# Second convolution with the propagation after the weights: transposes of the raw relu output in place of a matmul with S

## The chip, the cores and the metric

One core of one Trainium2 chip. The time is device time in microseconds (us), the median of several executions; a trace of one execution shows what each engine did. A core has TensorE (PE; its weight loads are PEld), VectorE (DVE), ScalarE (ACT), GpSimd (POOL) and queues for transfers. All data are FP32.

## The reference

128 graphs of 128 nodes with 512 features. Layer 0 is graph attention with a residual and a LayerNorm. Layer 1, cut to what the change touches:

```python
h = relu(hypergraph_conv(x, adj, W1, b1))        # 128 x 1024 per graph
h = layer_norm(h, gamma, beta)
y = hypergraph_conv(h, adj, W2, b2)              # 128 x 512
out = layernorm(x + (y + x))
# hypergraph_conv(x, adj, W, b) = D^-1 H B^-1 H^T (x W^T) + b
```

In the inputs gamma is one, and beta, b1 and b2 are zero.

## The kernel before

With S = H B^-1 H^T (symmetric, built once per graph) a convolution is D^-1 S (x W^T). The kernel multiplies by S first: a matmul with h as the stationary operand gives (S h)^T, which is just the layout that the product with the weights needs. The hidden layer is normalized on VectorE before that.

```python
def s7_hidden(g):
    ...                                   # ph = zT.T @ W1, h = relu(ph * D + b1)
    mv = moments(h, DH, f"h{g}")
    rs = rstd_of(mv[:, 1:2], f"h{g}")     # the power on GpSimd
    for q in range(2):                    # four VectorE passes per graph
        ... h = (h - mean) * gamma
        ... h = h * rs + beta

def s8_propagate(g):
    ...
        nc.tensor.matmul(p[:, k * N:(k + 1) * N], s["h"][:, c * P:(c + 1) * P], s["S"], ...)   # pu
    ...                                   # pu -> uT, half on ScalarE, half on VectorE

def s9_output(g):
    for k in range(KH):                   # py, 8 matmuls of 512 columns
        nc.tensor.matmul(p, s["uT"][:, k, :], w2_sb[:, k, :], ...)
    o = p * D + res; LayerNorm; store

order = (
    (s6_propagate, 2), (s4_transpose, 1), (s1_transpose, 0), (s7_hidden, 2),
    (s2_features, 0), (s3_softmax, 0), (s8_propagate, 2), (s5_attend, 1), (s9_output, 2),
)
for t in range(G + 2): ...                # stage(t - lag): three graphs in flight
```

Tile names in the traces: pz = x1 times S, pet, pt, pa = transposes, ph = first weights, pe, pd, pf = scores, S and features, ps = score matrix, pu = h times S, pav = attention, py = second weights.

## Time and profile before

| | before |
|---|---|
| time, median | 3494.22 us (3493.81 to 3496.34) |
| TensorE busy | 3447.3 us of 3493.5 |
| VectorE, ScalarE, GpSimd busy | 2251.0, 1203.7, 791.4 us |
| one loop step (start of one ph to the next) | 26.80 us |

The lines behind this stand in the prediction. A busy share of 99% does not say that nothing can be gained or lost on TensorE: the ends of matmul records are modelled and overlap the next ones. The distance between the starts of consecutive groups is what a stage costs.

### The profile page before, as it was taken

The page shows a single profiled execution, that of the slowest core. Times are in us where ns is not written, and L with a number is a line of the kernel's source. Part 1 is how long each engine was busy: PE and PEld are TensorE (multiplying, and loading weights), DVE is VectorE, ACT ScalarE, POOL GpSimd, SP SyncE. Part 2 cuts the span into 40 slices and gives each one's busy share as a digit, 9 for nine tenths or more (in the row PEclk, how much of TensorE's full clock was granted, in tenths as well). Part 3 has the DMA queues.
Part 4 walks back from the last instruction along what each step waited for, and adds up shares of the span by engine and source line. Part 5 has one row for each costly group of instructions (what it writes and reads, how often), then busy time and mean ns, then how long its engine had stood idle before and what let it go on. Part 6 is the DMA issues. An engine that isn't in the chain of part 4 may idle for free.

```text
span 3493.5 us, 39269 instructions
## 1 busy us (share of the span) xinstructions
PE 3447.3 (99%) x13952; PEld 1961.2 (56%) x13952; DVE 2251.0 (64%) x4880; ACT 1203.7 (34%) x3585; POOL 791.4 (23%) x910
## 2 busy tenths in 40 slices
PE   6999999999999999999999999999999999999998
PEld 3555555555555555555555555555555555555554
DVE  4666666666666666666666666666666666666664
ACT  2333333333333333333333333333333333333331
POOL 2222222222222222222222222222222222222221
PEclk9999999999999999999999999999999999999999
DMA  3000000000000000000000000000000000000000
GB/s 120 25 21 21 24 25 21 21 25 24 21 23 26 21 21 24 25 21 21 24 25 21 21 24 25 21 21 24 25 21 21 24 25 21 21 24 25 21 10 12
DMA packets 58596, 85.89 MB, mean 25 GB/s; under 512 B 6304, under 2 KB 22688, under 8 KB 58400
## 3 DMA queue, kind: packets, MB, share of 16 engines
q1 hardware_dynamic: 57392, 80.77, 7.0%
q8 instruction: 110, 1.80, 0.2%
q10 hardware_dynamic: 1008, 2.62, 0.2%
q14 instruction: 86, 0.70, 0.1%
HBM read 49.81 MB, written 33.55 MB: 24 GB/s over the span
## 4 chain that ended last, share of the span: by engine, by line
PE 98%; DVE 1%; DMA 0%; POOL 0%; ACT 0%; issue 0%; SPq 0%; POOLq 0%; DVEq 0%; ACTq 0%
PE py L340 25%; PE ph L299 25%; PE pf L204 13%; PE pu L326 7%; PE ps L217 7%; PE pav L262 6%; PE pe L181 4%; PE pz L285 3%; PE pet L251 3%; PE pt L154 2%; PE pd L191 2%; PE pd L192 0%; PE pa L156 0%; DMA w_sb<-in_w_dram 0%; DVE prod L114 0%
## 5 line engine op out<-in xcount | busy, mean ns | idle before, releaser
L340 PE MATMUL py<-w_sb,uT 128*128 128x512 f32 x2048 | 908.0, 596 | 0.0
L299 PE MATMUL ph<-w_sb,zT 128*128 128x512 f32 x2048 | 900.8, 593 | 0.7 <-ACT zT L290 0.7
L340 PEld LDWEIGHTS py<-w_sb,uT 128*128 128x128 f32 x2048 | 379.9, 191 | 429.2 <-issue 398.8
L299 PEld LDWEIGHTS ph<-w_sb,zT 128*128 128x128 f32 x2048 | 379.5, 190 | 429.8 <-issue 428.8
L204 PE MATMUL pf<-w_sb,xT 128*128 128x512 f32 x1024 | 473.7, 605 | 0.0
L302 DVE SCALAR_TENSOR_TENSOR h<-ph,D,b_bc 128x512 f32<-128x512 f32 x256 | 192.1, 751 | 430.4 <-PE ph L299 430.4
L239 ACT ACTIVATE e<-d,nmax 128x128 f32<-128x128 f32 x1024 | 396.1, 388 | 116.3 <-DVE nmax L232 116.3
L136 POOL TENSOR_TENSOR rs_h<-ve_h,mhalf 128x1 f32<-128x1 f32 x128 | 126.1, 985 | 1322.1 <-DVE ve_h L134 1322.1
L226 POOL TENSOR_TENSOR d<-d,neg 128x512 f32<-128x512 f32 x256 | 319.6, 1269 | 396.4 <-DVE D L199 365.9
L305 ACT ACTIVATE h<-h 128x512 f32<-128x512 f32 x256 | 161.1, 629 | 664.5 <-DVE h L302 664.5
L290 ACT COPY zT<-pz 128x512 f32<-128x512 f32 x128 | 75.0, 586 | 750.1 <-PE pz L285 750.1
L326 PEld LDWEIGHTS pu<-S,h 128*128 128x128 f32 x2048 | 241.5, 194 | 106.5 <-DVE dn L197 95.5
L144 DVE BATCH_NORM_STATS2 stats_h<-h 128x6 f32<-128x512 f32 x256 | 177.7, 694 | 178.0 <-ACT h L305 178.0
L204 PEld LDWEIGHTS pf<-w_sb,xT 128*128 128x128 f32 x1024 | 185.9, 192 | 185.3 <-issue 185.3
L326 PE MATMUL pu<-S,h 128*128 128x128 f32 x2048 | 266.0, 284 | 9.4 <-DVE h L314 9.4
L217 PE MATMUL ps<-rhs_aug,lhs_aug 40*128 40x512 f32 x512 | 253.5, 615 | 0.0
L262 PE MATMUL pav<-ft,eT 128*128 128x64 f32 x2048 | 243.5, 272 | 0.0
L262 PEld LDWEIGHTS pav<-ft,eT 128*128 128x128 f32 x2048 | 239.7, 193 | 0.8 <-PE ps L217 0.8
L225 DVE TENSOR_TENSOR d<-ps,d 128x512 f32<-128x512 f32 x256 | 176.9, 691 | 84.8 <-ACT d L224 71.8
L232 DVE TENSOR_REDUCE nmax<-d 128x4 f32<-128x512 f32 x256 | 175.5, 686 | 67.6 <-POOL d L226 67.6
L208 ACT COPY ft<-pf 128x512 f32<-128x512 f32 x128 | 74.9, 585 | 398.6 <-PE pf L204 398.6
L273 DVE SCALAR_TENSOR_TENSOR y<-y,x 128x512 f32<-128x512 f32 x128 | 88.6, 692 | 177.0 <-POOL y L272 177.0
(69 smaller groups left out, 3855.3 us busy)
## 6 DMA issues: line engine op xcount, KB each, us to landing
x<-in_x_dram SPq DMA_DIRECT2D x128, 256.0 KB, 2.6
out_dram<-o SPq DMA_DIRECT2D x128, 256.0 KB, 2.0
a<-in_adj_dram SPq DMA_DIRECT2D x128, 64.0 KB, 1.8
w_sb<-in_w1t_dram SPq DMA_DIRECT2D x1, 2048.0 KB, 13.9
w_sb<-in_w2t_dram SPq DMA_DIRECT2D x1, 2048.0 KB, 14.0
w_sb<-in_w_dram SPq DMA_DIRECT2D x1, 1024.0 KB, 11.3
b_bc<-in_b_dram ACTq DMA_DIRECT2D x2, 256.0 KB, 6.6
b_bc<-in_b_dram ACTq DMA_DIRECT2D x1, 512.0 KB, 8.5
```

Of the source, the lines that this page charges most:

```text
L144: nc.vector.bn_stats(stats[:, i, :], t[:, i * HALF:(i + 1) * HALF])
L204: nc.tensor.matmul(pf, s["xT"][:, k, :], w0_sb[:, k, :], start=(k == 0), stop=(k == KF - 1))
L217: nc.tensor.matmul(p, l, r[:, q * HH:(q + 1) * HH, :].rearrange("r h n -> r (h n)"), start=True, stop=True,)
L225: nc.vector.tensor_max(dq, ps[q], dq)
L226: nc.gpsimd.tensor_tensor(d[:, q * HH:(q + 1) * HH, :], d[:, q * HH:(q + 1) * HH, :], s["neg"][:, None, :].to_broadcast([P, HH, N]), op=AL ...
L232: nc.vector.tensor_reduce(nmax[:, q * HH:(q + 1) * HH], d[:, q * HH:(q + 1) * HH, :], AX.X, ALU.max, negate=True,)
L239: nc.scalar.activation(e[:, h, :], d[:, h, :], AF.Exp, bias=nmax[:, h:h + 1], accum_out=den[:, h:h + 1])
L262: nc.tensor.matmul(p[:, h * U:(h + 1) * U], s["eT"][:, h, :], s["ft"][:, h * U:(h + 1) * U], start=True, stop=True,)
L299: nc.tensor.matmul(p, s["zT"][:, k, :], w1_sb[:, k, cols], start=(k == 0), stop=(k == KF - 1))
L302: nc.vector.scalar_tensor_tensor(h[:, cols], p, s["D"], b1_bc[:, cols], op0=ALU.mult, op1=ALU.add)
L326: nc.tensor.matmul(p[:, k * N:(k + 1) * N], s["h"][:, c * P:(c + 1) * P], s["S"], start=True, stop=True,)
L340: nc.tensor.matmul(p, s["uT"][:, k, :], w2_sb[:, k, :], start=(k == 0), stop=(k == KH - 1))
```

## The change

The intent: take the LayerNorm of the hidden layer off the path to TensorE. With per-row mean mu and factor rs,

S LN(h) W2 = (S diag(rs)) (h (gamma W2) - mu (gamma^T W2)) + (S 1) (beta^T W2).

So the raw relu output is transposed, multiplied by w2g = gamma W2, corrected by a rank-one term for the mean (y2), and multiplied by Sr = diag(rs) S (S is symmetric) only then (pq). The beta term goes into the residual. gamma^T W2 and beta^T W2 are made once by TensorE (pv) and spread over the partitions through DRAM. The core of the diff:

```diff
 def s2_features(g):
-    nc.scalar.copy(sm, pd[:, :N])
+    nc.scalar.activation(sm, pd[:, :N], AF.Copy, accum_out=ssum)
+    nc.vector.tensor_mul(dsum, ssum, dd)
 def s5_attend(g):
-    nc.vector.scalar_tensor_tensor(res, x1, 2.0, b2_bc, op0=ALU.mult, op1=ALU.add)
+    nc.gpsimd.tensor_scalar(res, bw_bc, s["dsum"], None, op0=ALU.mult)
+    nc.gpsimd.tensor_tensor(res, res, b2_bc, op=ALU.add)
+    nc.vector.scalar_tensor_tensor(res, x1, 2.0, res, op0=ALU.mult, op1=ALU.add)
 def s7_hidden(g):
-    (four VectorE passes over h, 128 x 512 each)
+    nc.vector.tensor_scalar(nmu, mv[:, 0:1], -1.0, None, op0=ALU.mult)
+    nc.gpsimd.tensor_scalar(sr, s["S"], rs, None, op0=ALU.mult)
 (second convolution)
-    nc.tensor.matmul(p[...], s["h"][:, c * P:(c + 1) * P], s["S"], ...)      # pu, 8 per graph
+    nc.tensor.transpose(p[...], s["h"][:, c * P:(c + 1) * P], ident)         # pu, 8 per graph
-    nc.tensor.matmul(p, s["uT"][:, k, :], w2_sb[:, k, :], ...)               # py, 8 per graph
+    nc.tensor.matmul(p, s["hTh"][:, k, :], w2g[:, k, :], ...)                # py, 8 per graph
+    nc.vector.scalar_tensor_tensor(y2, gw_bc, s["nmu"], p, op0=ALU.mult, op1=ALU.add)
+    nc.tensor.matmul(p, s["Sr"], s["y2"], start=True, stop=True)             # pq, 1 per graph
-    (s6_propagate, 2), (s4_transpose, 1), (s1_transpose, 0), (s7_hidden, 2), ...
+    (s6_propagate, 2), (s10_output, 3), (s4_transpose, 1), (s1_transpose, 0), (s7_hidden, 2), ...
+    (fold(), pv and w2g, at the end of the first step)
```

More of the change, by code (lines that the diff above doesn't have):

```diff
@@ L60 @@
     work = ctx.enter_context(tc.tile_pool(name="work", bufs=2))
-    small = ctx.enter_context(tc.tile_pool(name="small", bufs=4))
+    small = ctx.enter_context(tc.tile_pool(name="small", bufs=6))
+    dram = ctx.enter_context(tc.tile_pool(name="dram", bufs=1, space=bass.MemoryType.DRAM))
     psum = ctx.enter_context(tc.tile_pool(name="psum", bufs=8, space=bass.MemoryType.PSUM))
@@ L95 @@
     b1_bc = spread(b1, DH, "b1_bc")
-    g_bc = spread(gamma, DH, "g_bc")
-    be_bc = spread(beta, DH, "be_bc")
     b2_bc = spread(b2, F, "b2_bc")
+    gb = const.tile([P, 2, KH], F32, name="gb")
+    for c, ap in ((0, gamma), (1, beta)):
+        nc.scalar.dma_start(gb[:, c, :], ap.rearrange("(k p) -> p k", p=P))
     load(2)
@@ L147, in moments, with fold @@
         return mv
+    w2g = const.tile([P, KH, F], F32, name="w2g")
+    gw_bc = const.tile([P, F], F32, name="gw_bc")
+    bw_bc = const.tile([P, F], F32, name="bw_bc")
+    def fold():
+        pv = bank("pv")
+        for k in range(KH):
+            nc.tensor.matmul(
+                pv[:2], gb[:, :, k], w2_sb[:, k, :], start=(k == 0), stop=(k == KH - 1)
+            )
+        sums = const.tile([2, F], F32, name="sums")
+        nc.vector.tensor_copy(sums, pv[:2])
+        sums_d = dram.tile([2, F], F32, tag="sums_d", name="sums_d")
+        nc.scalar.dma_start(sums_d, sums)
+        for c, t in ((0, gw_bc), (1, bw_bc)):
+            nc.scalar.dma_start(t, sums_d[c].partition_broadcast(P))
+        for k in range(KH):
+            nc.gpsimd.tensor_scalar(w2g[:, k, :], w2_sb[:, k, :], gb[:, 0, k:k + 1], None, op0=ALU.mult)
     def s1_transpose(g):
@@ L193, in s2_features @@
         sm = s["S"] = work.tile([P, N], F32, tag="S", name=f"S_{g}", bufs=4)
-        nc.scalar.copy(sm, pd[:, :N])
+        ssum = small.tile([P, 1], F32, tag="ssum", name=f"ssum_{g}")
+        nc.scalar.activation(sm, pd[:, :N], AF.Copy, accum_out=ssum)
         dn = small.tile([P, 1], F32, tag="dn", name=f"dn_{g}")
@@ L201, in s2_features @@
         )
+        dsum = s["dsum"] = small.tile([P, 1], F32, tag="dsum", name=f"dsum_{g}")
+        nc.vector.tensor_mul(dsum, ssum, dd)
         pf = bank(f"pf_{g}")
@@ L277, in s5_attend @@
         nc.vector.tensor_scalar(x1, y, mv[:, 0:1], rs, op0=ALU.subtract, op1=ALU.mult)
-        res = s["res"] = work.tile([P, F], F32, tag="res", name=f"res_{g}")
-        nc.vector.scalar_tensor_tensor(res, x1, 2.0, b2_bc, op0=ALU.mult, op1=ALU.add)
+        res = s["res"] = work.tile([P, F], F32, tag="res", name=f"res_{g}", bufs=4)
+        nc.gpsimd.tensor_scalar(res, bw_bc, s["dsum"], None, op0=ALU.mult)
+        nc.gpsimd.tensor_tensor(res, res, b2_bc, op=ALU.add)
+        nc.vector.scalar_tensor_tensor(res, x1, 2.0, res, op0=ALU.mult, op1=ALU.add)
     def s6_propagate(g):
@@ L306, in s7_hidden, with s8_transpose @@
         mv = moments(h, DH, f"h{g}")
+        nmu = s["nmu"] = small.tile([P, 1], F32, tag="nmu", name=f"nmu_{g}")
+        nc.vector.tensor_scalar(nmu, mv[:, 0:1], -1.0, None, op0=ALU.mult)
         rs = rstd_of(mv[:, 1:2], f"h{g}")
-        for q in range(2):
-            cols = slice(q * HALF, (q + 1) * HALF)
-            nc.vector.scalar_tensor_tensor(
-                h[:, cols], h[:, cols], mv[:, 0:1], g_bc[:, cols],
-                op0=ALU.subtract, op1=ALU.mult,
-            )
-            nc.vector.scalar_tensor_tensor(
-                h[:, cols], h[:, cols], rs, be_bc[:, cols], op0=ALU.mult, op1=ALU.add
-            )
-    def s8_propagate(g):
+        sr = s["Sr"] = work.tile([P, N], F32, tag="Sr", name=f"Sr_{g}")
+        nc.gpsimd.tensor_scalar(sr, s["S"], rs, None, op0=ALU.mult)
+    def s8_transpose(g):
         s = st[g]
-        uT = s["uT"] = work.tile([P, KH, N], F32, tag="uT", name=f"uT_{g}")
+        hT = s["hTh"] = work.tile([P, KH, N], F32, tag="hTh", name=f"hTh_{g}")
         per = HALF // N
@@ L325, in s8_propagate @@
                 c = q * per + k
-                nc.tensor.matmul(
-                    p[:, k * N:(k + 1) * N], s["h"][:, c * P:(c + 1) * P], s["S"],
-                    start=True, stop=True,
+                nc.tensor.transpose(
+                    p[:, k * N:(k + 1) * N], s["h"][:, c * P:(c + 1) * P], ident
                 )
-            dst = uT[:, q * per:(q + 1) * per, :].rearrange("p k n -> p (k n)")
+            dst = hT[:, q * per:(q + 1) * per, :].rearrange("p k n -> p (k n)")
             if q:
@@ L334, in s8_propagate, with s9_weights, s10_output @@
                 nc.scalar.copy(dst, p)
-    def s9_output(g):
-        s = st.pop(g)
-        p = bank(f"py_{g}")
-        for k in range(KH):
-            nc.tensor.matmul(
-                p, s["uT"][:, k, :], w2_sb[:, k, :], start=(k == 0), stop=(k == KH - 1)
-            )
+    def s9_weights(g, half):
+        s = st[g]
+        if half == 0:
+            s["py"] = bank(f"py_{g}")
+        p = s["py"]
+        for k in range(half * KH // 2, (half + 1) * KH // 2):
+            nc.tensor.matmul(
+                p, s["hTh"][:, k, :], w2g[:, k, :], start=(k == 0), stop=(k == KH - 1)
+            )
+        if half == 0:
+            return
+        y2 = s["y2"] = work.tile([P, F], F32, tag="y2", name=f"y2_{g}")
+        nc.vector.scalar_tensor_tensor(y2, gw_bc, s["nmu"], p, op0=ALU.mult, op1=ALU.add)
+    def s10_output(g):
+        s = st.pop(g)
+        p = bank(f"pq_{g}")
+        nc.tensor.matmul(p, s["Sr"], s["y2"], start=True, stop=True)
         o = work.tile([P, F], F32, tag="o", name=f"o_{g}", bufs=3)
@@ L351 @@
     order = (
-        (s6_propagate, 2), (s4_transpose, 1), (s1_transpose, 0), (s7_hidden, 2),
-        (s2_features, 0), (s3_softmax, 0), (s8_propagate, 2), (s5_attend, 1), (s9_output, 2),
+        (s6_propagate, 2), (s10_output, 3), (s4_transpose, 1), (s1_transpose, 0), (s7_hidden, 2),
+        (s2_features, 0), (s3_softmax, 0), (s8_transpose, 2), (s5_attend, 1),
+        (lambda g: s9_weights(g, 0), 2), (lambda g: s9_weights(g, 1), 2),
     )
-    for t in range(G + 2):
+    for t in range(G + 3):
         if AHEAD <= t + AHEAD - 1 < G:
@@ L360 @@
                 stage(t - lag)
+        if t == 0:
+            fold()
 def kernel(
```

## The prediction

> **What bounds the kernel now.** I read the page's busy shares first, then the chain of work that ended last, then one loop step of the timeline, engine by engine.
>
> ```profile
> PE 3447.3 (99%) x13952; PEld 1961.2 (56%) x13952; DVE 2251.0 (64%) x4880; ACT 1203.7 (34%) x3585; POOL 791.4 (23%) x910
> ...
> PE 98%; DVE 1%; DMA 0%; POOL 0%; ACT 0%; issue 0%; SPq 0%; POOLq 0%; DVEq 0%; ACTq 0%
> ```
>
> TensorE is busy 99% of the span and 98% of the chain. VectorE has 36% to spare, so what the change takes from it (four 745 ns passes per graph) buys nothing by itself. The price is set by TensorE's order and its waits. One step of the loop (one graph enters, one leaves), TensorE's rows, columns start, length, line, operation, count:
>
> ```profile
> 1734.48 1.98 PE L217 MATMUL ps<-rhs_aug,lhs_aug 40*128 40x512 f32 x4
> 1736.39 2.05 PE L326 MATMUL pu<-S,h 128*128 128x128 f32 x16
> 1738.28 1.90 PE L262 MATMUL pav<-ft,eT 128*128 128x64 f32 x16
> 1740.02 7.08 PE L340 MATMUL py<-w_sb,uT 128*128 128x512 f32 x16
> 1746.94 1.05 PE L285 MATMUL pz<-S,x 128*128 128x128 f32 x8
> 1747.83 1.04 PE L251 MATMUL pet<-ident,e 128*128 128x128 f32 x8
> 1748.70 0.60 PE L154 MATMUL pt<-ident,x 128*128 128x128 f32 x4
> 1749.14 0.27 PE L156 MATMUL pa<-ident,a 128*128 128x128 f32 x1
> 1749.25 7.03 PE L299 MATMUL ph<-w_sb,zT 128*128 128x512 f32 x16
> ```
>
> Read starts, not lengths: lengths overlap, because each includes the time until the last result is out. The previous step's ph row starts at 1722.45, so a step is 26.80 us, with no gap in it. Start to start: ps 1.91, pu 1.89, pav 1.74, py 6.92, pz 0.89, pet 0.87. A matmul is two records (pu: 8 matmuls, x16), a transpose is one (pet: 8 transposes, x8). That is the saving that the change is after.
>
> VectorE in the same step, around the end of py:
>
> ```profile
> 1744.77 0.55 DVE L277 TENSOR_SCALAR x<-y,mv_a,rs_a 128x512 f32<-128x512 f32 x1 [0.66 <-POOL rs_a L136]
> 1745.35 0.69 DVE L279 SCALAR_TENSOR_TENSOR res<-x,b_bc 128x512 f32<-128x512 f32 x1
> 1747.14 0.75 DVE L344 SCALAR_TENSOR_TENSOR o<-py,D,res 128x512 f32<-128x512 f32 x1 [1.09 <-PE py L340]
> ```
>
> The py bank can be read 0.20 us after pz has begun (1747.14 less 1746.94), and the pass takes 0.75 us.
>
> The tail, where no other graph covers the hidden layer's chain (TensorE rows):
>
> ```profile
> 3449.15 3.75 PE L326 MATMUL pu<-S,h 128*128 128x128 f32 x16 [4.74 <-DVE h L314]
> 3452.70 2.56 PE L262 MATMUL pav<-ft,eT 128*128 128x64 f32 x16
> 3455.09 7.09 PE L340 MATMUL py<-w_sb,uT 128*128 128x512 f32 x16
> ```
>
> Here TensorE stands 4.74 us behind the normalization and then runs pu at half speed (3.75 against 2.05 us). This happens for the last two graphs only.
>
> **What the Trainium skill says.** "TensorE: Matmul & The Clock Gate", section "Back-to-back issue gap", gives N/2.4 + 2.5 ns between warm matmuls. "FP8 and Floating Point Precision", section "TensorE Precision Notes", says that true FP32 takes four passes. Together they fit the trace: two records per matmul, each streaming its columns twice, make 1024/2.4 + 2.5 = 429 ns per record, and py shows 6.92/16 = 433. The first page's section "Step-by-step: what each phase is for" says that weight loads are pulled ahead of running matmuls. The trace agrees where nothing is waited for: pz's first load starts at 1746.51, before the last py record has ended. After a wait it does not: in the tail, ph waits for zT; its load and its first record both start at 3463.80 and the third load comes 0.54 us later instead of 0.43, so 0.11 us of load is exposed. Last, "Part 4: PE-mode transpose" of that page says that transposes do not count as busy for the clock. The trace does not contradict this, but its three transpose groups in a row (1.42 us) leave the granted clock at 1.00 in every steady window.
>
> **The change part by part, per step.**
> Removed: 8 matmuls h times S, 1.89 us. Added in the same place: 8 transposes. Pace as pet, 0.87, plus the first weight load behind ps, which is exposed there: 16 records at pz's pace (0.89 per 8) would be 1.78, pu takes 1.89, so 0.11. Sum 0.98. Difference -0.91 us.
> Kept: py, 8 matmuls of 512 columns, 6.92 us (w2g in place of w2).
> Added: pq, one matmul of 512 columns, two records: 6.92/8 = +0.865 us. TensorE's own balance is thus about zero, -0.05 us.
> Added: a new wait. The instruction order puts pq directly behind pz, and pq needs y2, a VectorE pass over the finished py bank. Counting from the start of pz: bank readable 0.20, pass 0.75, restart of TensorE 0.06 (zT ends 3463.74, ph's load 3463.80), exposed load 0.11: pq streams from 1.12 us. Without the wait it would stream from 0.89. +0.23 us.
> VectorE is free for y2: x1 and res hang on ps, not on py, and end 11.56 us after ps starts (1746.04 less 1734.48). In the new step py starts 0.91 us earlier; its bank is readable 1.91 + 0.98 + 1.74 + 6.92 + 0.20 = 11.75 us after ps. The slack is 0.19 us, thin.
> pz needs x1 at 11.55 after ps and gets it at 10.84: no wait.
> Hidden: VectorE loses 4 x 0.745 us and gains y2 (0.75) and two small operations (0.15 each); it should fall from 2251 to about 2030 us. GpSimd gains res (a 128x512 multiply, about 0.7 us, estimated from 297 ns for 128x128 and 1027 ns for 1024 columns; an add, 1.27) and Sr (0.30): about +2.25 us per step, to some 1080 us. They run between the hidden layer's variance (1733.1) and the masking adds (1737.0); chained they end at about 1736.1, so they fit. ScalarE's accumulation with S adds about 0.3 us, off the path.
> Step: -0.91 + 0.865 + 0.23 = +0.185 us. Over some 126 steps: +23 us.
> Start: the fold is 8 matmuls of 512 columns, 6.9 us, where TensorE now waits 3.2 us for the first softmax: about +4. The sums' round trip through DRAM also holds GpSimd's queue, because the first res waits for it ahead of the first masking and bias adds, so it may be more. 1 MB less of broadcasts while the first weights load gives perhaps 1 back. I take +4 us.
> Tail: the waits of 4.74 and 4.65 us shrink to about 1.2 each (h pass 0.75, relu 0.63, less the first bank's transposes): -7. The half-clock stretches behind them (pu 3.75 and 3.79 against 1.89, py 7.95 against 6.92, pav 0.6) go: -5.4. The last pq stands behind a fully exposed y2: +0.9 beyond what is counted. About -11.5 us.
> Sum: 3494 + 23 + 4 - 11.5 = 3509.5 us.
>
> **Rivals.**
> (a) The y2 wait is hidden, because TensorE takes up pq without exposing its load or because the bank is readable earlier. For it: only 0.06 us separates y2's end (0.95) from pz's end (0.89). Against: every stalled start in the tail shows the exposed load. Then a step is 26.75 us, and the time about 3481 us.
> (b) VectorE is late for y2: res now also waits for GpSimd, and the slack is 0.19 us. If GpSimd's three new operations push the masking adds back by 0.5 us, y2 starts about 0.3 us late: +38 us, 3547 us. Against: GpSimd is idle for 2.90 us just before those adds in the trace.
> (c) The waits that the change removes are worth more than I think: nothing in a steady step waits for the normalization now, so there is nothing to win except in the tail. I give this little.
> (d) More transposes pull the clock down. One stretch like the tail's pu (3.75 us for 1.89 us of work) in every step would cost 7%. Against: the new group lies between ps and pav, alone, 0.98 us.
>
> **Range and chances.** (a) to my sum spans 3481 to 3510; part of (b), and a start of +10, reach 3530. I predict 3509 us, 8 in 10 between 3488 and 3531. Two per cent is 70 us, or 0.55 us per step: no saving of that size exists on TensorE, so faster gets 0.01. Slower needs (b) in full and more, or (d): 0.03. Within 2%: 0.96.
>
> **What would show it.** Transposes at one record each, a step between two pu rows 0.98 us long up to pav; pz to pq 1.1 us from start to start; pq to pet about 0.97 or 0.87 (whether the exposed load is booked to pq or ahead of it); a step of 26.95 to 27.05. TensorE's busy share may hide the wait, since pz's last record is drawn until 1.05 us after its start. Waits in the tail of about 1 us for h. If pz to pq is 0.89, (a) holds; if y2 starts later than 0.25 us after pz, (b).

## The result, and the profile after

| | before | after |
|---|---|---|
| time, median | 3494.22 us | 3514.31 us (3513.83 to 3514.95, 4 runs) |
| span of the profiled run | 3493.5 us | 3512.0 us |
| one loop step (mean of 125) | 26.80 us | 27.02 us |
| VectorE busy | 2251.0 us | 1984.3 us |
| GpSimd busy | 791.4 us | 1184.3 us |

The ratio is 1.0057, 95% interval 1.0043 to 1.0071; the ratios quoted here are those of the medians quoted. The change takes 267 us of work off VectorE and makes the kernel 0.6% slower: clear of the noise, and within the 2% below which two kernels count as the same.

The page of the changed kernel, busy shares and chain of work:

```profile
PE 3462.8 (99%) x13200; PEld 1884.8 (54%) x13200; DVE 1984.3 (56%) x4753; ACT 1228.4 (35%) x3713; POOL 1184.3 (34%) x1302
...
PE 98%; issue 1%; DMA 0%; DVE 0%; POOL 0%; ACT 0%; POOLq 0%; ACTq 0%
```

TensorE is again 99% busy. New is 1% of "issue" in the chain: time that the profile puts down to nobody. One step of the timeline, TensorE:

```profile
1752.55 1.09 PE L351 MATMUL pu<-ident,h 128*128 128x128 f32 x8
1753.48 1.90 PE L289 MATMUL pav<-ft,eT 128*128 128x64 f32 x16
1755.21 7.08 PE L366 MATMUL py<-w2g,hTh 128*128 128x512 f32 x16
1762.13 1.05 PE L315 MATMUL pz<-S,x 128*128 128x128 f32 x8
1763.28 1.10 PE L377 MATMUL pq<-y,Sr 128*128 128x512 f32 x2
1764.21 1.04 PE L278 MATMUL pet<-ident,e 128*128 128x128 f32 x8
```

Start to start: pu now takes 0.93 us (1.89 before). pz has the same 8 records as before and takes 1.14 to 1.15 us to its follower, where it took 0.89. pq takes 0.93 us up to pet. No bracket marks a wait on these rows, because pz's last record is drawn until 1763.18, only 0.10 us before pq. The Trainium skill says in "Perfetto Trace Analysis", section "Tensor Engine Instruction (MATMUL, LD_WEIGHTS)", that a TensorE end time is estimated and not observed; here that estimate covers most of a wait of 0.25 us per step. The same place with all engines:

```profile
1761.78 0.69 DVE L309 SCALAR_TENSOR_TENSOR res<-x,res 128x512 f32<-128x512 f32 x1
1762.13 1.05 PE L315 MATMUL pz<-S,x 128*128 128x128 f32 x8
...
1762.39 0.74 DVE L372 SCALAR_TENSOR_TENSOR y<-gw_bc,nmu,py 128x512 f32<-128x512 f32 x1
1763.25 0.30 PEld L377 LDWEIGHTS pq<-y,Sr 128*128 128x128 f32 x2 [0.25 <-issue]
1763.28 1.10 PE L377 MATMUL pq<-y,Sr 128*128 128x512 f32 x2
```

The DVE row "y<-gw_bc" is y2. It begins 0.26 us after pz, with VectorE coming straight from res, and ends at 1763.13. Only then, 0.12 us later, does pq's weight load begin, though its operand Sr was ready long before. The wait for y2 is not on the matmul but on a separate semaphore instruction ahead of the load (51 ns, from 0.04 us after y2's end in the packed trace), so that the load is held back with the matmul. In the kernel before, the load of a group that waits for nothing stands ahead of the group (pz's at 1746.51 for 1746.94).

GpSimd in the same step:

```profile
1750.02 0.61 POOL L341 TENSOR_SCALAR Sr<-S,rs_h 128x128 f32<-128x128 f32 x1
1750.60 1.56 POOL L307 TENSOR_SCALAR res<-bw_bc,dsum 128x512 f32<-128x512 f32 x1
1752.25 1.27 POOL L308 TENSOR_TENSOR res<-res,b_bc 128x512 f32<-128x512 f32 x1
1753.48 2.50 POOL L253 TENSOR_TENSOR d<-d,neg 128x512 f32<-128x512 f32 x2
```

The masking adds (tile d) in the kernel before:

```profile
1737.04 2.49 POOL L226 TENSOR_TENSOR d<-d,neg 128x512 f32<-128x512 f32 x2 [2.90 <-DVE D L199]
```

Before, GpSimd stood idle for 2.90 us ahead of them and began them 2.56 us after ps. Now its three new operations run up to them, and they begin 2.84 us after ps (1750.64). The run res_plain below, without the two res rows, starts them at 2.56 again.

The tail, TensorE. ph and pu of the last two graphs are no longer separated by the normalization:

```profile
3474.47 0.60 PE L351 MATMUL pu<-ident,h 128*128 128x128 f32 x4
3476.33 0.66 PE L351 MATMUL pu<-ident,h 128*128 128x128 f32 x4 [1.26 <-ACT h L335]
3476.82 1.90 PE L289 MATMUL pav<-ft,eT 128*128 128x64 f32 x16
```

The wait is 1.26 us instead of 4.74 (and again 1.26 for the last graph, instead of 4.65), and the half-speed stretch behind it is gone; the granted clock was 0.50 in it before (3449.1 to 3452.5).

Where the 18.5 us between the two profiled spans (3493.5 and 3512.0) come from, all read from starts of ph rows: the first ph starts at 60.16 us before and 63.06 after (+2.9); from there to the ph of the third graph from the end it is 3350.84 us (to 3411.00) and 3378.06 us (to 3441.12), which is +27.2 over 125 steps; from there to the end 82.5 and 70.9 us (-11.6).

### The profile page after: what moved, and what is told of

The parts are those of the page before. It is cut to its first block, busy times and chain, and to the rows that moved or that the text cites. A ratio compares the mean times of both kernels' runs of the same rounds, so it can differ in the third digit from the quotient of the medians.

```text
span 3512.0 us, 38412 instructions
## 1 busy us (share of the span) xinstructions
PE 3462.8 (99%) x13200; PEld 1884.8 (54%) x13200; DVE 1984.3 (56%) x4753; ACT 1228.4 (35%) x3713; POOL 1184.3 (34%) x1302
## 4 chain that ended last, share of the span: by engine, by line
PE 98%; issue 1%; DMA 0%; DVE 0%; POOL 0%; ACT 0%; POOLq 0%; ACTq 0%
PE py L366 25%; PE ph L329 25%; PE pf L231 13%; PE ps L244 7%; PE pav L289 6%; PE pq L377 4%; PE pu L351 4%; PE pe L205 4%; PE pz L315 3%; PE pet L278 3%; PE pt L178 2%; PE pd L215 2%; PE pd L216 0%; PE pa L180 0%; PE pv L161 0%
## 5 line engine op out<-in xcount | busy, mean ns | idle before, releaser
L366 PE MATMUL py<-w2g,hTh 128*128 128x512 f32 x2048 | 906.9, 596 | 0.0
L366 PEld LDWEIGHTS py<-w2g,hTh 128*128 128x128 f32 x2048 | 379.3, 190 | 428.5 <-issue 428.1
L139 POOL TENSOR_TENSOR rs_h<-ve_h,mhalf 128x1 f32<-128x1 f32 x128 | 70.3, 549 | 1150.1 <-DVE dn L222 1134.0
L139 POOL TENSOR_TENSOR rs_o<-ve_o,mhalf 128x1 f32<-128x1 f32 x128 | 70.3, 550 | 737.4 <-DVE ew L190 716.9
L299 POOL TENSOR_TENSOR y<-y,b_bc 128x512 f32<-128x512 f32 x128 | 162.5, 1270 | 128.3 <-DVE y L294 128.1
L307 POOL TENSOR_SCALAR res<-bw_bc,dsum 128x512 f32<-128x512 f32 x128 | 200.2, 1564 | 5.1 <-DMA bw_bc<-sums_d 5.1
```

Of the source, the lines that this page charges most:

```text
L307: nc.gpsimd.tensor_scalar(res, bw_bc, s["dsum"], None, op0=ALU.mult)
L366: nc.tensor.matmul(p, s["hTh"][:, k, :], w2g[:, k, :], start=(k == 0), stop=(k == KH - 1))
```

## The experiments

Theory 1: the loss is the wait of pq for y2, together with the weight load that this wait exposes, in the place where pq stands; without it the change would gain. Rivals: pq costs its 1.2 us wherever it stands; or GpSimd's new work is what delays y2 and is the whole loss.

**pq_later.** The same kernel, pq two groups later:

```diff
-    (s6_propagate, 2), (s10_output, 3), (s4_transpose, 1), (s1_transpose, 0), (s7_hidden, 2),
+    (s6_propagate, 2), (s4_transpose, 1), (s1_transpose, 0), (s10_output, 3), (s7_hidden, 2),
```

> The last propagation (pq) moves from behind pz to behind the transposes of x and adj, so that y2 has 2.3 us from the start of pz instead of 0.9. Theory 1 (the loss is the wait for y2, with the weight load that it exposes): pz to its follower falls from 1.14 to 0.89 us, pq costs 0.87 instead of 0.93, the step falls from 27.03 to 26.71 us, the time by 126 x 0.32 = 40 us to about 3474 us, below the kernel before. Rival (pq costs its 1.2 us wherever it stands, through its own operand load or its place in the PSUM rotation): step 27.0, 3514 us.

Measured: 3473.87 us, against 3494.18 for the kernel before on the same chip (ratio 0.9942, 0.9925 to 0.9958). TensorE in one step:

```profile
1743.30 1.05 PE L315 MATMUL pz<-S,x 128*128 128x128 f32 x8
1744.19 1.04 PE L278 MATMUL pet<-ident,e 128*128 128x128 f32 x8
1745.07 0.60 PE L178 MATMUL pt<-ident,x 128*128 128x128 f32 x4
1745.50 0.27 PE L180 MATMUL pa<-ident,a 128*128 128x128 f32 x1
1745.61 1.02 PE L377 MATMUL pq<-y,Sr 128*128 128x512 f32 x2
1746.47 7.03 PE L329 MATMUL ph<-w_sb,zT 128*128 128x512 f32 x16
```

pz takes 0.89 again, pq 0.86, the step 26.70 us (the ph before starts at 1719.77). Moving pq (with the VectorE passes of the output, which wait for it) behind 1.4 us of other work gives 40 us and turns a loss of 0.6% into a gain of 0.6%. The rival on pq's own cost falls. So the wait costs 0.32 us per step: 0.25 between pz and pq, 0.07 as a slower start of pq.

**res_plain.** The two GpSimd operations of the residual are left out (res = 2 x1 + b2 again). This is right with these inputs, because beta is zero, and wrong in general.

```diff
-    nc.gpsimd.tensor_scalar(res, bw_bc, s["dsum"], None, op0=ALU.mult)
-    nc.gpsimd.tensor_tensor(res, res, b2_bc, op=ALU.add)
-    nc.vector.scalar_tensor_tensor(res, x1, 2.0, res, op0=ALU.mult, op1=ALU.add)
+    nc.vector.scalar_tensor_tensor(res, x1, 2.0, b2_bc, op0=ALU.mult, op1=ALU.add)
```

> GpSimd's two operations for the residual are left out (res = 2 x1 + b2 again; right here because beta is zero, wrong in general). pq keeps its place. Theory 1: GpSimd delays y2 by only 0.05 us per step, so pz to pq falls from 1.14 to about 1.09 us and the time by some 6 us, plus about 4 us at the start, because the first residual no longer waits for the sums' round trip: 3504 us. Rival 2 (GpSimd's backlog is the whole wait): pz to pq falls to 0.89 us, the time to about 3478 us.

Measured: 3505.74 us (ratio to before 1.0033), so 8.6 us less than the change. VectorE and TensorE at pq:

```profile
1730.41 1.05 PE L313 MATMUL pz<-S,x 128*128 128x128 f32 x8
...
1730.62 0.75 DVE L370 SCALAR_TENSOR_TENSOR y<-gw_bc,nmu,py 128x512 f32<-128x512 f32 x1 [0.16 <-PE py L364]
1731.48 0.30 PEld L375 LDWEIGHTS pq<-y,Sr 128*128 128x128 f32 x2 [0.20 <-issue]
1731.51 1.10 PE L375 MATMUL pq<-y,Sr 128*128 128x512 f32 x2
```

y2 now waits for py itself (0.16 us) and starts 0.21 us after pz; pz to pq is 1.10 us. GpSimd's backlog is worth 0.04 us per step (1.14 to 1.10), 4.4 us over the 125 steps, and the first ph starts at 60.18 instead of 63.06 us. Together that is the 7.3 us by which the two profiled spans differ. As the whole cause this rival falls: 0.21 of the 0.25 us stay.

**sr_vector.** Sr on VectorE, so that pq waits for one engine only.

```diff
-    nc.gpsimd.tensor_scalar(sr, s["S"], rs, None, op0=ALU.mult)
+    nc.vector.tensor_scalar(sr, s["S"], rs, None, op0=ALU.mult)
```

> Sr is made on VectorE instead of GpSimd, so pq waits for one engine instead of two; res stays on GpSimd. Theory 1: the second wait costs a separate semaphore instruction of 0.05 us, and GpSimd's masking adds come 0.6 us earlier, which takes away the 0.05 us by which y2 is late: pz to pq about 1.03 us instead of 1.14, 12 to 14 us in all, about 3501 us. Rival: the semaphore instruction runs ahead and costs nothing, then pz to pq stays at 1.09 and the time at about 3508 us.

Measured: 3501.22 us (ratio to before 1.0020). TensorE at pq:

```profile
1729.56 1.05 PE L315 MATMUL pz<-S,x 128*128 128x128 f32 x8
...
1730.56 0.30 PEld L377 LDWEIGHTS pq<-y,Sr 128*128 128x128 f32 x2
1730.56 1.12 PE L377 MATMUL pq<-y,Sr 128*128 128x512 f32 x2
1731.52 1.04 PE L278 MATMUL pet<-ident,e 128*128 128x128 f32 x8
```

y2 starts 0.20 us after pz (1729.76) and ends at 1730.51; the load follows 0.05 us later. In res_plain it follows 0.11 us after y2's end (1731.37). The difference is the separate semaphore instruction, which the traces show once per pq (128 of 51 ns each) with two waits, and not with one; here the wait for y2 is on the load itself. The exposed weight load stays: pq takes 0.96 us here up to pet, 0.10 more than in pq_later. The gain has two parts: y2 begins 0.05 us earlier (without Sr ahead of them, GpSimd's masking adds begin 2.65 and not 2.84 us after ps), and the hand-over from y2's end to the load is 0.06 us shorter. What is left of the wait is 0.21 us: this run has the conditions that the prediction assumed, and it put the wait at 0.23.

**y2_twice.** The suspected wait lengthened: VectorE copies y2 onto itself once more before pq may read it.

```diff
     nc.vector.scalar_tensor_tensor(y2, gw_bc, s["nmu"], p, op0=ALU.mult, op1=ALU.add)
+    nc.vector.tensor_copy(y2, y2)
```

> y2 is copied onto itself on VectorE once more before pq may read it (0.55 to 0.6 us). If the wait for y2 stands in the path one to one, the step grows by that much, to about 27.6 us, and the time by 70 to 76 us, to about 3588 us. If TensorE had slack at pq, the time stays at 3514 us.

Measured: 3572.57 us, one look, +58.3. The size was missed, because the copy takes 0.43 us, not 0.55. pz to pq grows from 1.14 to 1.60, by 0.46; 126 times that is 58 us. The slope is the one that theory 1 asks for: y2's chain lies on the path one to one.

**no_pq.** One part of the change alone, with a wrong result: the output is taken from y2 without the last propagation.

```diff
-    p = bank(f"pq_{g}")
-    nc.tensor.matmul(p, s["Sr"], s["y2"], start=True, stop=True)
+    p = s["y2"]
```

> Wrong result on purpose: the last propagation is left out, the output is taken from y2 directly. What remains of the change on TensorE is transposes in place of h times S. Theory 1: the step is 27.03 - 1.14 - 0.93 + 0.89 = 25.85 us, 0.95 below the kernel before, and the time about 3514 - 126 x 1.18 - 2 = 3363 us: TensorE sets the step alone, and the change gives the whole saving back for one 512-column matmul and its wait. Rival: with TensorE relieved, the chain over VectorE and GpSimd (y, x1, res), which already delays the first weight load of pz, becomes the bound, and the step stays above 26.2 us (over 3405 us).

Measured: 3364.05 us (one look), step 25.84 us. The transposes save 0.96 us per step, and nothing but TensorE binds down to a step of 25.84 us: against the 27.02 us of the changed kernel the other engines have at least 1.18 us to spare. In the correct kernel pq takes 0.86 of these 0.96 back by its own work alone.

**row_terms_vector.** Towards a better version: pq in the late place, the beta row and rs in a second VectorE pass over y2, S itself as pq's operand; GpSimd loses Sr and both residual operations.

```diff
     nc.vector.scalar_tensor_tensor(y2, gw_bc, s["nmu"], p, op0=ALU.mult, op1=ALU.add)
+    nc.vector.scalar_tensor_tensor(y2, y2, s["rsh"], bw_bc, op0=ALU.mult, op1=ALU.add)
-    nc.tensor.matmul(p, s["Sr"], s["y2"], start=True, stop=True)
+    nc.tensor.matmul(p, s["S"], s["y2"], start=True, stop=True)
```

> pq behind the transposes, as in the run before with that place; and the two row terms go to VectorE: y2 gets a second pass (times rs, plus the beta row), S itself is the operand, GpSimd loses Sr and both residual operations. y2 is ready about 1.7 us after the start of pz, pq starts at 2.3: the step stays at 26.71 us. The start loses GpSimd's wait for the sums, first ph at about 60 instead of 63.6 us: about 3471 us.

Measured: 3472.79 us (ratio to before 0.9939), step 26.70 us, first ph at 60.57 us. The second pass costs nothing in a step.

**fold_in_gap.** The same as row_terms_vector, with the fold one step later and w2g on ScalarE (two changes at once; no run separates them):

```diff
-    nc.gpsimd.tensor_scalar(w2g[:, k, :], w2_sb[:, k, :], gb[:, 0, k:k + 1], None, op0=ALU.mult)
+    nc.scalar.activation(w2g[:, k, :], w2_sb[:, k, :], AF.Copy, scale=gb[:, 0, k:k + 1])
-        if t == 0:
+        if t == 1:
             fold()
```

> As the run before, and the fold of gamma and beta moves one step later, into the wait of TensorE for the first x1, with w2g made on ScalarE. Step 26.71 us again. The pv products fill a wait of 6 to 9 us and keep the clock up: first ph at about 58.8 us or a little earlier, 3467 to 3469 us, 0.7% below the kernel before. If the fold did not matter to the start, it stays at 3471 us.

Measured: 3469.15 us against 3494.00 (ratio 0.9929, 0.9916 to 0.9943, 5 rounds); it beats both kernels. TensorE's start in row_terms_vector, and then in this one:

```profile
48.02 2.00 PE L286 MATMUL pav<-ft,eT 128*128 128x64 f32 x16
55.93 2.08 PE L310 MATMUL pz<-S,x 128*128 128x128 f32 x8 [5.91 <-DVE x L301]
```

```profile
45.96 2.00 PE L286 MATMUL pav<-ft,eT 128*128 128x64 f32 x16
47.89 7.03 PE L161 MATMUL pv<-w_sb,gb 128*2 128x512 f32 x16
54.85 1.16 PE L310 MATMUL pz<-S,x 128*128 128x128 f32 x8
```

The fold's 7 us of matmuls fill the wait for the first x1, pz follows at once and at full speed (1.16 against 2.08 us; granted clock 1.00 against 0.50), and the first ph starts at 57.26 instead of 60.57 us. Of these 3.3 us, 1.1 are the earlier start of pz and 2.2 the faster rows between it and ph.

## Why the prediction was right

It was right in sign and in its cause for the step, and close in size: 3509 us predicted, 3514.31 measured, within 2%, to which it gave 0.96. Part of the closeness is luck, as said below. Its terms:

| term, us | predicted | measured |
|---|---|---|
| pu to transposes, per step | -0.91 | -0.96 (1.89 to 0.93; no_pq: 26.80 to 25.84) |
| pq's own work | +0.865 | +0.86 (pq_later) |
| wait for y2, with the exposed load | +0.23 | +0.32 (0.25 + 0.07) |
| step | +0.185 | +0.22 (27.2 us over 125 steps) |
| start | +4 | +2.9 |
| tail | -11.5 | -11.6 |

- The transposes: the first weight load behind ps, which the prediction added as 0.11 us, costs 0.06 (0.93 against pet's 0.87).
- The wait was the term that was mis-sized, by 0.09 us per step or about 11 us. Three pieces, as means of the steady steps: y2 ends 0.10 us after the 0.89 us of pz, put at 0.06, because it begins at 0.25 and not 0.20 (res_plain gives back 0.04); the load follows y2's end by 0.12 us, put at 0.06, because the second wait adds a semaphore instruction, which the prediction left out (0.06 between res_plain and sr_vector); the exposed load is 0.10, put at 0.11.
- The two errors in the step go opposite ways (the wait +0.09, the transposes -0.05), so that about half of the first is hidden in the sum. That is luck.
- That y2 begins late is rival (b) in a small size. The prediction estimated the GpSimd multiply at 0.7 us and Sr at 0.30, from an operation with constant factors (297 ns) and a copy (1027 ns). With a factor per row they take 1.56 and 0.61 us, and GpSimd's total came to 1184 us, not 1080. So the three operations did not fit into GpSimd's gap, and the slack of 0.19 us on VectorE was used up. As the whole cause rival (b) fell (res_plain). The sum for VectorE has a slip: its own terms give 2251 - 128 x 1.93 = 2004 us, not 2030; measured are 1984.
- Rival (a), the wait hidden, is not what happened where pq stood, and is what happens two groups later: step 26.70, a little below its 26.75.
- Rival (c): nothing was won in a steady step by taking the normalization off the path; the tail is the only place, as predicted. Rival (d), a lower clock: the granted clock was 1.00 in all steady windows of the changed kernel.
- The start was put at +4, for the fold's matmuls in TensorE's path, and was +2.9 for another reason; this is luck too. In res_plain the fold is unchanged and the first ph starts at 60.18, as before the change (60.16): the fold costs nothing net there. The 2.9 us are the residual's work on GpSimd, which the prediction named only as a risk of more: it waits for the sums from DRAM ahead of the masking adds, and then takes 5.6 us itself for two graphs.

```profile
46.23 3.10 POOL L307 TENSOR_SCALAR res<-bw_bc,dsum 128x512 f32<-128x512 f32 x2 [5.07 <-DMA bw_bc<-sums_d]
```

- The tail holds piece by piece: the two waits put at about 1.2 us are 1.26 each, and the last pq waits 0.93 us for y2, put at 0.9.

What stays open: where the 0.05 us between the predicted and the measured transposes come from, and why pq's exposed load is booked partly ahead of its first record (0.03) and partly to pq (0.07). Both are below what these runs tell apart.

## What to carry to other kernels

Where one engine is at 99%, count what a change does to that engine's own rows first: here a transform that frees VectorE of 267 us, and per graph swaps 16 short TensorE records for 8 short and 2 long ones, is about even, and the place of one new dependent instruction decides the sign. An instruction that needs another engine's answer to the product just finished belongs behind enough independent work to cover that answer, the hand-over and its own operand load; here 1.4 us more were worth 40 us over 128 graphs. Read such waits from start to start, because a short one hides under the drawn end of the record before it.

## What the Trainium skill lacked or had wrong

- "TensorE: Matmul & The Clock Gate", section "Step-by-step: what each phase is for", tells of weight loads that run ahead; it lacks that the wait for a matmul's moving operand can stand on its weight load (sr_vector) or ahead of it (the changed kernel), so that the load is held back too. Here Sr was ready, only y2 was awaited, and the load began 0.05 us after y2's end (sr_vector); this exposes 0.10 us (pq 0.96 against 0.86).
- The same page, section "Terms", gives its transpose mode as 4 times faster for FP32. Eight 128x128 FP32 transposes took 0.93 us in place of eight matmuls in 1.89: a factor of 2. This does not refute the page: each transpose also needs a weight load (8 loads against 16), and no run here shows which of the two sets the pace, or that nc.tensor.transpose uses this mode.
- No page has the price of a second awaited engine on a TensorE instruction ("Perfetto Trace Analysis", section "Identifying Dependency Chains", only names the instruction that may be inserted for it): one semaphore instruction of 51 ns, and the load 0.11 instead of 0.05 us after the last of the two.
- "GPSIMD Engine Reference", section "3.1 Elementwise — side-by-side cycle accounting", lacks a multiply by a factor per row: 1564 ns for 128x512 and 612 ns for 128x128, more than the 1277 ns of a two-tensor add of 128x512 and twice the 298 ns of a 128x128 operation with constants.
